# Attention values stored unscaled and loaded by pairs of heads, in a kernel of two graph-attention layers

## The chip, the cores and the metric

The kernel runs on one core of one Trainium2 chip. The metric is the device time of one execution in microseconds (us), lower is better. The profile is that of one execution; its span is a little shorter than the timed figure.

## The reference, cut to what matters

For each of B = 8 batches of N = 2048 nodes with D = 256 features there are two layers. Layer 0 has H = 8 heads of DH = 32 features:

```python
x_proj = einsum('bnd,hdf->bhnf', x, W)
e = leaky_relu(e_src[..., :, None] + e_dst[..., None, :], 0.2) + beta * log(prior + EPS)
e = where(adj > 0, e, neg_inf)
h = einsum('bhij,bhjf->bhif', softmax(e, axis=-1), x_proj)   # heads joined to 256 features
x = layernorm(x + h @ W_out.T)
```

Here `prior` is the adjacency matrix itself. Layer 1 takes `h1 = x W1`, `h2 = x W2`, `h3 = x W3`, scores `h1 h2^T` with a leaky relu, the same mask and a softmax, and ends with `layernorm(x + relu(attention h3))`.

## The kernel before, in words

**Layer 0** (class `Gat`, one object for each batch) turns the softmax into products. With the sender score split into two exponentials, kept as the factors `re` (two for each node and head), and a query row `c` for each head, the unnormalised weight of sender j for all 2048 receivers is one VectorE instruction, `s = max(c, re0[j]) * mt[j]` (L374), times a factor `re1[j]`. `mt` is a row of the transposed mask and prior, 1 MB for a tile of 128 senders. Before the change the factor `re1` is multiplied into the values v in advance (`scale`, L290 to L294: one instruction for four tiles of senders, four for a batch); the denominators take it as the weight of their product.

The work of a batch is 64 steps (`step`, L350): four pairs of heads `hp`, and in each 16 tiles of senders `jt`. A step makes two scores tiles s (buffers for two steps), and then the matrix products, L406, `val += v^T s` and `den += re1^T s`, each 16 matmuls in the profile. The denominators can also be summed on the other engines: for the tiles in the table `SUMMED` (L68, the chain of a pair) the first is copied times its factor to `d` by ScalarE (L391), the others are added on VectorE in the next step, two instructions for a tile (L385), and one product with ones brings `d` into `den` at the pair's last tile. The `d` tiles have two buffers, which the odd `mt` rows of batch 0 and its reciprocals `rb` also use.

`finish` (L410 on) copies a pair's sums out, takes reciprocals `rc`, sends them through memory (`rec_d`), reads them back spread over partitions (`rb`, L442) and multiplies (L448). `output` (L451) makes the rows of layer 0's result (`y`, L475, added to the input rows `xg` on VectorE at L477), and `turn` transposes them for layer 1.

**Layer 1** (class `Dot`) takes the rows in 16 steps of 128 (`step`, L547): scores `e` (L536), the mask on VectorE (L541), an exponential on ScalarE (L544), transposes `pt` (L559) copied to `pts` by ScalarE (L561), and the product `acc` (L575). For batch 0 it makes the mask rows `pen` from the adjacency matrix (`adj_r`, L213) and stores them; later batches load them.

**The order.** Batch 0's 64 attention steps run first, and between them the projections of batches 2, 3, 4, 5, 1, 6, 7 (`others`, L605): 16 rows a batch, in groups of four, `row` (L265) with a ScalarE copy into v (L272). After a batch's last row come its `factors` (L276) and its first `scale`, the other three at the next turns of the loop; the profile shows them close together. Batches 2 to 7 then store v as one 2 MB transfer (`store`, L296); batch 1 keeps its v in SBUF. After that, for each batch b, the attention steps of b + 1 are woven with layer 1 of b by an order written out by hand (L670 on): the last two dot steps of the batch before, with steps 0 to 5 of the new batch; the output rows and their turning, with steps 6 to 15; then 14 dot steps with the rest. At the head of a batch its v comes back in four loads (`load`, L308), into one buffer of 16 KB a partition, so after the last val product of the batch before.

TensorE's order is the program's from the start, SyncE's (SP, which issues nearly all loads and stores, in order) from L668 on. VectorE and ScalarE take their instructions in an order that the scheduler fixes at compile time, near that of the program. The `mt` rows are loaded two steps ahead (`load_ahead`, L324). The buffers `ht` (three, 4 KB a partition) hold in turn `adj_r`, `dn`, `rb`, `xg`, the transposed input `xt` and `h1`.

Of the kernel before, what the change touches and what calls it, by code (L numbers as in the profile page):

```python
# [18 lines left out]
P = 128  # L19
# [8 lines left out]
def kernel(  # L28
# [38 lines left out]

    SUMMED = [[()] * NP, [(9, 11, 13)] + [(0, 3, 6, 8, 11, 14)] * (NP - 1)]  # L68
    SUMMED += [[(8, 10, 12, 14)] + [tuple(range(0, NT, 2))] * (NP - 1)] * (B - 2)

# [88 lines left out]
    c_d = dram.tile([B, H, N], F32, name="c_d")  # L159
    v_d = dram.tile([B, P, NT, D], F32, name="v_d")  # L160
    re_d = dram.tile([B, P, 2, NT, H], F32, name="re_d")
# [43 lines left out]
    def mask(it, make):  # L205

        pen = wide_tile("pen", "pen", 1, BF16)
        if not make:
            nc.sync.dma_start(pen, pen_d[ts(it, P), :])
            return pen  # L210
        for s in range(2):
            a = chunk.tile([P, HALF], I32, tag="ht", name="adj_r", bufs=3)
            nc.sync.dma_start(a, adj[ts(it, P), ts(s, HALF)])  # L213
            nc.vector.tensor_scalar(pen[:, ts(s, HALF)], a, 0.0, NO_EDGE, ALU.is_le, ALU.mult)
        return pen
# [18 lines left out]
    class Gat:  # L234


        def __init__(self, b):
            self.b = b
            self.units = ((hp, jt) for hp in range(NP) for jt in range(NT))
            self.ms, self.mts = [], []  # L240
            self.later = gats[b - 1].later if b > 0 else []

        def begin(self, kept):


            self.v = whole.tile([P, NT, D], F32, tag=kept, name="v")
            self.both = small.tile([P, NT, 2 * H], F32, name="both", bufs=2)
# [16 lines left out]

        def row(self, it, xt, scores=True):  # L265

            cols = D + 2 * H if scores else D
            t = mm_tile("proj")
            for kc in range(KC):
                nc.tensor.matmul(t[:, 0:cols], xt[:, kc, ts(it % IG, P)], wp[:, kc, 0:cols],  # L270
                                 start=(kc == 0), stop=(kc == KC - 1))
            nc.scalar.copy(self.v[:, it, :], t[:, 0:D])  # L272
            if scores:
                nc.scalar.copy(self.both[:, it, :], t[:, D:cols])
# [14 lines left out]

        def scale(self, g):  # L290

            v = self.v[:, ts(g, IG), :].rearrange("p t (h f) -> p (t h) f", f=DH)
            e = self.re[:, 1, ts(g, IG), :].rearrange("p t h -> p (t h)")
            nc.vector.tensor_tensor(v, v, e.unsqueeze(2).to_broadcast([P, IG * H, DH]), ALU.mult)  # L294

        def store(self):  # L296
            nc.sync.dma_start(v_d[self.b], self.v)
            nc.sync.dma_start(re_d[self.b], self.re)

# [7 lines left out]

        def load(self):  # L308
            self.v = whole.tile([P, NT, D], F32, name="v")
            for g in range(NB):  # L310
                nc.sync.dma_start(self.v[:, ts(g, IG), :], v_d[self.b, :, ts(g, IG), :])
                yield

# [10 lines left out]
        def load_ahead(self):  # L324


            self.mt_loads = (load_mt(jt, False) for _ in range(self.b, B) for _ in range(NP) for jt in range(NT))
            self.c_loads = (gats[b].query_rows(h) for b in range(self.b, B) for h in range(H))
            self.mts, self.cs_ahead = [], []
            for _ in range(2):  # L330
                self.cs_ahead.append(next(self.c_loads))
                self.mts.append(next(self.mt_loads))
            self.cs_ahead.append(next(self.c_loads))

# [12 lines left out]
        def step(self, count=1):  # L347

            for _ in range(count):
                hp, jt = next(self.units)  # L350
                for work in list(self.later):
                    if next(work, self) is self:
                        self.later.remove(work)
                if self.b > 0 and hp == NP - 1 and jt == 0 and self.b + 1 < B:
                    gats[self.b + 1].load_factors()
                if jt == 0:
                    if self.b > 0:
                        self.cs = [self.cs_ahead.pop(0) for _ in range(HP)]
                    else:
                        self.cs = [self.query_rows(hp * HP + a) for a in range(HP)]  # L360
                    self.val = pacc.tile([P, HALF], F32, tag="val", name="val")
                    self.den = pacc.tile([P, HALF], F32, tag="den", name="den")
# [8 lines left out]
                for a in range(HP):  # L371
# [4 lines left out]
                    if self.b > 0 and jt == NT - 1:  # L376
                        self.cs_ahead += [c for c in [next(self.c_loads, None)] if c]
                if self.b > 0:
                    self.mts += [t for t in [next(self.mt_loads, None)] if t]
                v, e = self.v, self.re[:, 1]  # L380
                heads = [hp * HP + a for a in range(HP)]
# [4 lines left out]
                self.last = s  # L386
                self.products(self.val, [v[:, jt, ts(h, DH)] for h in heads], s, jt == 0, jt == NT - 1)
                if jt in chain[:1]:
# [21 lines left out]
        def finish(self, hp):  # L410
# [7 lines left out]
            for s in range(2):  # L418
                nc.scalar.copy(ht[lo:lo + HP * DH, ts(s, NT // 2), :],
                               self.val[ts(s, HP * DH), :].rearrange("p (t i) -> p t i", i=P))  # L420
            dn = chunk.tile([P, HALF], F32, tag="ht", name="dn", bufs=3)
            nc.scalar.copy(dn, self.den)
# [13 lines left out]
            for s in range(2):  # L436
                if b == 0:
                    rb = wide_tile("rb", "d", 2)[:, 0:HALF]
                else:
                    rb = chunk.tile([P, HALF], F32, tag="ht", name="rb", bufs=3)  # L440
                for a in range(2 * HP):
                    nc.sync.dma_start(rb[ts(a, DH), :],  # L442
                                      rec_d[b, hp // 2, s, a // HP, a % HP:a % HP + 1, :].to_broadcast([DH, HALF]))
                rbs.append(rb)
                yield
# [5 lines left out]
        def output(self):  # L451
# [6 lines left out]
            def load(g):  # L458
                xs.append(chunk.tile([P, IG, D], F32, tag="ht", name="xg", bufs=3))
                nc.sync.dma_start(xs[g], xb[:, ts(g, IG), :])  # L460

            load(0)
            yield
            for g in range(NB):
                if g < NB - 1:
                    load(g + 1)

# [45 lines left out]
    class Dot:  # L513
# [7 lines left out]
        def queries(self, g):  # L521
            self.h1 = h1 = chunk.tile([P, KC, BK], F32, tag="ht", name="h1", bufs=3)
            for dc in range(KC):
# [65 lines left out]
    g0 = gats[0]  # L589
    g0.begin("x1t")  # L590
    xt0 = whole.tile([P, KC, N], F32, tag="heads", name="xt0")
# [4 lines left out]
    for g in range(NB):  # L596
        for k in range(IG):
            g0.row(g * IG + k, xt0[:, :, ts(g, BK)], False)
        g0.scale(g)
        if g == 0:  # L600
            g0.queries()
        elif g == 1:
            g0.more_mt(1)

    def others():  # L605


# [8 lines left out]
        def turn(n):  # L616
            if n < len(groups):
                xts.append(chunk.tile([P, KC, BK], F32, tag="ht", name="xt", bufs=3))
                transpose_x(xgs[n], xts[n])
                load(n + 1)  # L620
# [4 lines left out]
        for n, (gat, g) in enumerate(groups):  # L625
            if g == 0:
                if gat is order[-1]:

                    for _ in range(IG):
                        if scaling:  # L630
                            scaling.pop(0)()
                        yield
                gat.begin("h3" if n // NB % 2 or gat is order[-1] else "v")
            for k in range(IG):
                gat.row(g * IG + k, xts[n])
                if k == 1:
                    turn(n + 1)
                if g == NB - 1 and k == IG - 1:
                    gat.factors()
                    gat.scale(0)  # L640
                    scaling.extend([lambda gat=gat, i=i: gat.scale(i) for i in range(1, NB)])
                    if gat.b > 1:
                        scaling.append(gat.store)
                if g == 0 and k == IG - 1 and n > 0:
                    groups[n - 1][0].queries()
                yield
        order[-1].queries()
        yield

    scaling = []  # L650
    projections, weights = others(), later_weights()
    next(projections)
    count = (B - 1) * NT + IG
    for k in range(1, NP * NT + 1):
# [3 lines left out]
        if k % 2 == 0:  # L658
            for _ in range(k * count // (NP * NT) - (k - 2) * count // (NP * NT)):
                next(projections)  # L660
            if scaling:
                scaling.pop(0)()
            if k > NT:
# [6 lines left out]
    for b in range(1, B + 1):  # L670
# [6 lines left out]
        if b > 1 and fresh:  # L677
            fresh.follow(gat)
            values = fresh.load()
            next(values)  # L680
            fresh.later.append(values)
        rows, turns = gat.output(), gat.turn()
        if dot is None:
            for _ in range(4):
                layer_0(1)
                if scaling:
                    scaling.pop(0)()
            next(projections)
# [61 lines left out]
```

## Time and profile before

Three timed runs took 4340.97 to 4343.44 us, median 4342.68. The profiled execution has a span of 4341.2 us and took 4343.01.

| Engine | busy us | share of the span |
|---|---|---|
| TensorE (PE) | 4208.8 | 97% |
| TensorE weight loads (PEld) | 2204.3 | 51% |
| VectorE (DVE) | 3717.5 | 86% |
| ScalarE (ACT) | 1664.9 | 38% |

| Group of instructions | count | busy us | mean ns of one |
|---|---|---|---|
| L374 s, DVE | 1024 | 2355.9 | 2344 |
| L406 val, PE | 8192 | 1043.5 | 604 |
| L385 d, DVE | 322 | 747.8 | 2343 |
| L406 den, PE (weights `re`) | 5168 | 667.1 | 597 |
| L391 d, ACT | 56 | 112.3 | 2012 |
| L294 v scaled, DVE | 32 | 37.8 | 1220 |

A mean of one instruction is from its start to its end; PE's matmuls are pipelined and overlap, so their mean is longer than their share of the engine. SP issues 496 loads of `mt` of 1 MB, six stores of v of 2 MB and 24 loads of v of 0.5 MB; the DMA engines move 839.04 MB, 193 GB/s over the span.

### The profile page before, as it was taken

What the parts mean: (1) busy time and instruction counts of PE and PEld (TensorE: products, weight loads), DVE (VectorE), ACT (ScalarE), POOL (GpSimd) and SP (SyncE); (2) the same over time, 40 slices, a digit from 0 to 9 for tenths busy, and PEclk for the clock granted to TensorE, in tenths of its full rate; (3) what the DMA queues carried; (4) which work ended last, traced back from release to release, by engine and by line L of the source; (5) the groups of instructions that cost most, each with busy time, mean ns of one, the idle gap of its engine ahead of it and who ended that gap; (6) DMA issues with size and microseconds to landing.
All of it is one profiled execution on the core that took longest, in us unless ns stands there. A gap on an engine that the chain in (4) does not pass through costs nothing. (4 is left out here: it accounts for less than half of the span.)

```text
span 4341.2 us, 58763 instructions
## 1 busy us (share of the span) xinstructions
PE 4208.8 (97%) x24608; PEld 2204.3 (51%) x24608; DVE 3717.5 (86%) x2472; ACT 1664.9 (38%) x3021; POOL 9.5 (0%) x14
## 2 busy tenths in 40 slices
PE   7999899999999999999999999999999999999999
PEld 4444345454555545555455554555455545555766
DVE  6888788898899988999899988999899988999222
ACT  6522143233343324333443333333334333333554
POOL 0000000000000000000000000000000000000000
PEclk9999999999999999999999999999999999999999
DMA  8877665566555564556555465556545565544211
GB/s 250 291 262 278 219 229 199 195 228 236 188 188 187 191 231 156 194 186 223 200 184 180 181 232 180 188 192 218 205 166 187 186 229 182 195 177 146 80 50 40
DMA packets 253162, 839.04 MB, mean 193 GB/s; under 512 B 32224, under 2 KB 150752, under 8 KB 178400
## 3 DMA queue, kind: packets, MB, share of 16 engines
q1 hardware_dynamic: 217568, 801.71, 52.3%
q10 hardware_dynamic: 35328, 33.56, 2.3%
q8 instruction: 193, 3.16, 0.3%
q14 instruction: 73, 0.60, 0.0%
HBM read 761.53 MB, written 73.14 MB: 192 GB/s over the span
## 5 line engine op out<-in xcount | busy, mean ns | idle before, releaser
L374 DVE SCALAR_TENSOR_TENSOR s<-c,re,mt 128x2048 f32<-128x2048 f32 x1024 | 2355.9, 2344 | 126.7 <-PE den L406 70.7
L406 PE MATMUL val<-s,v 128*32 128x512 f32 x8192 | 1043.5, 604 | 72.9 <-DVE s L374 72.6
L575 PE MATMUL acc<-h,pts 128*128 128x256 f32 x4096 | 955.3, 381 | 11.6 <-ACT pts L561 11.4
L536 PE MATMUL e<-x1t,h 128*128 128x512 f32 x2048 | 904.0, 594 | 4.3 <-ACT pts L561 4.2
L575 PEld LDWEIGHTS acc<-h,pts 128*128 128x128 f32 x4096 | 746.9, 190 | 110.0 <-ACT pts L561 24.4
L385 DVE SCALAR_TENSOR_TENSOR d<-s,re,d 128x2048 f32<-128x2048 f32 x322 | 747.8, 2343 | 0.0
L406 PE MATMUL den<-s,re 128*32 128x512 f32 x5168 | 667.1, 597 | 0.0
L536 PEld LDWEIGHTS e<-x1t,h 128*128 128x128 f32 x2048 | 379.0, 190 | 451.3 <-issue 414.0
L406 PEld LDWEIGHTS val<-s,v 128*32 128x32 f32 x8192 | 246.6, 110 | 709.6 <-issue 517.5
L561 ACT COPY pts<-pt 128x512 f32<-128x512 f32 x512 | 296.7, 583 | 721.8 <-PE pt L559 717.1
L538 ACT ACTIVATE p<-e 128x512 f32<-128x512 f32 x512 | 302.4, 595 | 418.4 <-PE e L536 406.6
L541 DVE CUSTOM_DVE_ANT_0 p<-p,pen 128x2048 f32<-128x2048 f32 x128 | 292.7, 2287 | 186.7 <-ACT p L538 186.2
L406 PEld LDWEIGHTS den<-s,re 128*32 128x32 f32 x5168 | 183.4, 111 | 393.9 <-issue 389.9
L559 PEld LDWEIGHTS pt<-ident,p 128*128 128x128 f32 x2048 | 238.5, 141 | 214.4 <-issue 173.1
L544 ACT ACTIVATE p<-p,neg 128x2048 f32<-128x2048 f32 x128 | 256.7, 2005 | 211.9 <-DVE neg L541 211.9
L559 PE MATMUL pt<-ident,p 128*128 128x128 f32 x2048 | 317.7, 278 | 0.0
L580 ACT ACTIVATE z<-acc,rec 128x256 f32<-128x256 f32 x128 | 60.6, 474 | 385.2 <-PE acc L575 258.8
L581 DVE TENSOR_TENSOR z<-z,x1r 128x256 f32<-128x256 f32 x128 | 54.0, 422 | 154.2 <-ACT z L580 154.2
L270 PE MATMUL proj<-wp,xt 128*128 128x272 f32 (+1 forms) x512 | 130.9, 401 | 3.4 <-ACT v L272 2.3
L272 ACT COPY v<-proj 128x256 f32<-128x256 f32 x128 | 46.9, 376 | 206.9 <-PE proj L270 193.0
L391 ACT ACTIVATE d<-s,re 128x2048 f32<-128x2048 f32 x56 | 112.3, 2012 | 33.3 <-DVE s L374 18.3
L506 PE MATMUL h3p<-w3s,x1t 128*128 128x256 f32 x512 | 122.3, 382 | 1.8 <-ACT x1t L501 1.6
(88 smaller groups left out, 1916.2 us busy)
## 6 DMA issues: line engine op xcount, KB each, us to landing
mt<-mt_d SPq DMA_DIRECT2D x496, 1024.0 KB
c<-c_d SPq DMA_DIRECT2D x64, 1024.0 KB
pen<-pen_d SPq DMA_DIRECT2D x112, 512.0 KB
xg<-in_x_dram SPq DMA_DIRECT2D x60, 512.0 KB
adj_t<-in_adj_dram SPq DMA_DIRECT2D x16, 1024.0 KB
mt_d<-mt SPq DMA_DIRECT2D x16, 1024.0 KB
rb<-rec_d SPq DMA_DIRECT2D x128, 128.0 KB
x_d<-ht ACTq DMA_DIRECT2D x32, 512.0 KB
```

Source lines behind the costliest of these rows:

```text
L270: nc.tensor.matmul(t[:, 0:cols], xt[:, kc, ts(it % IG, P)], wp[:, kc, 0:cols], start=(kc == 0), stop=(kc == KC - 1))
L374: nc.vector.scalar_tensor_tensor(sa, self.cs[a], self.re[:, 0, jt, h:h + 1], mt, ALU.max, ALU.mult)
L385: nc.vector.scalar_tensor_tensor(d, sa, e[:, jt - 1, h:h + 1], d, ALU.mult, ALU.add)
L406: nc.tensor.matmul(dst[ts(q, DH), ts(c, BK)], weights[q % 2], s[q % 2][:, ds(q // 2 * HALF + c * BK, BK)], start=start, stop=stop)
L506: nc.tensor.matmul(t[:, ts(i, D)], x1t[:, kc, ts(2 * (j - lag) + i, P)], w3s[:, kc, :], start=(kc == 0), stop=(kc == KC - 1))
L536: nc.tensor.matmul(t, self.h1[:, kc, ts(it % IG, P)], self.x1t[:, kc, ts(c, BK)], start=(kc == 0), stop=(kc == KC - 1))
L538: nc.scalar.activation(p[:, ts(c, BK)], t, AF.Prelu, alpha=ALPHA)
L541: nc.vector.tensor_tensor_reduce(p, p, pen, -1.0, FMAX, ALU.add, ALU.min, neg)
L544: nc.scalar.activation(p, p, AF.Exp, bias=neg, scale=-1.0, accum_out=den)
L559: nc.tensor.transpose(t[:, ts(k, P)], p[:, ts(g * IG + k, P)], ident)
L561: nc.scalar.copy(pt, t)
L575: nc.tensor.matmul(acc, now[:, ts(k, P)], self.h3[:, j, :], start=(j == 0), stop=(j == NT - 1))
```

## The change

The values stay unscaled when they are made. All of batches 1 to 7 are stored group by group (0.5 MB for four tiles, in the layout pair, node, tile, feature) and their factors too; the values come back by pairs of heads (0.5 MB each), at tile 4 of the pair in front, and are scaled in one instruction at tile 12 of it. Batch 0's stay in SBUF in the new layout: its first pair is scaled before the steps start, the others at tile 12 of the pair in front. The value tiles are now 4 KB a partition with three buffers; the 4 KB saved are a fourth `ht` buffer, and `output` loads its input rows two groups ahead. The chain of the first pair is taken away for batch 1 and lies on tiles 2, 4, 10, 13 for batches 2 to 7. In batch 1's first pair the odd `mt` rows go into the two `d` buffers, so that up to four rows are ahead.

```diff
-    SUMMED = [[()] * NP, [(9, 11, 13)] + [(0, 3, 6, 8, 11, 14)] * (NP - 1)]
-    SUMMED += [[(8, 10, 12, 14)] + [tuple(range(0, NT, 2))] * (NP - 1)] * (B - 2)
+    SUMMED = [[()] * NP, [()] + [(0, 3, 6, 8, 11, 14)] * (NP - 1)]
+    SUMMED += [[(2, 4, 10, 13)] + [tuple(range(0, NT, 2))] * (NP - 1)] * (B - 2)
...
-    v_d = dram.tile([B, P, NT, D], F32, name="v_d")
+    v_d = dram.tile([B, NP, P, NT, HP * DH], F32, name="v_d")
...
-            a = chunk.tile([P, HALF], I32, tag="ht", name="adj_r", bufs=3)
+            a = chunk.tile([P, HALF], I32, tag="ht", name="adj_r", bufs=4)
...
-            nc.scalar.copy(self.v[:, it, :], t[:, 0:D])
+            nc.scalar.copy(v, t[:, 0:D].rearrange("p (h f) -> p h f", h=NP))
...
-        def scale(self, g):
-
-            v = self.v[:, ts(g, IG), :].rearrange("p t (h f) -> p (t h) f", f=DH)
-            e = self.re[:, 1, ts(g, IG), :].rearrange("p t h -> p (t h)")
-            nc.vector.tensor_tensor(v, v, e.unsqueeze(2).to_broadcast([P, IG * H, DH]), ALU.mult)
-
-        def store(self):
-            nc.sync.dma_start(v_d[self.b], self.v)
-            nc.sync.dma_start(re_d[self.b], self.re)
+        def scale(self, hp):
+
+            v = self.v[hp].rearrange("p t (a f) -> p t a f", a=HP)
+            e = self.re[:, 1, :, ts(hp, HP)]
+            nc.vector.tensor_tensor(v, v, e.unsqueeze(3).to_broadcast([P, NT, HP, DH]), ALU.mult)
...
-        def load(self):
-            self.v = whole.tile([P, NT, D], F32, name="v")
-            for g in range(NB):
-                nc.sync.dma_start(self.v[:, ts(g, IG), :], v_d[self.b, :, ts(g, IG), :])
-                yield
+        def load(self, hp):
+            self.v[hp] = chunk.tile([P, NT, HP * DH], F32, tag="v", name="v", bufs=3)
+            nc.sync.dma_start(self.v[hp], v_d[self.b, hp])
...
-            self.mt_loads = (load_mt(jt, False) for _ in range(self.b, B) for _ in range(NP) for jt in range(NT))
+            self.mt_loads = (load_mt(jt, b == self.b and hp == 0)
+                             for b in range(self.b, B) for hp in range(NP) for jt in range(NT))
...
+                at = self.b * NP + hp + 1
+                if at < B * NP:
+                    gat = gats[at // NP]
+                    if jt == 4 and gat.b > 0:
+                        gat.load(at % NP)
+                    elif jt == 12:
+                        gat.scale(at % NP)
...
-                if self.b > 0:
+                if self.b > 0 and len(self.mts) < (4 if not SUMMED[self.b][hp] and jt < NT - 4 else 2):
                     self.mts += [t for t in [next(self.mt_loads, None)] if t]
...
             load(0)
+            load(1)
             yield
             for g in range(NB):
-                if g < NB - 1:
-                    load(g + 1)
+                if g < NB - 2:
+                    load(g + 2)
...
+                if k == IG - 1:
+                    nc.sync.dma_start(v_d[gat.b].rearrange("h p t f -> p h t f")[:, :, ts(g, IG), :], v)
                 if g == NB - 1 and k == IG - 1:
                     gat.factors()
-                    gat.scale(0)
-                    scaling.extend([lambda gat=gat, i=i: gat.scale(i) for i in range(1, NB)])
-                    if gat.b > 1:
-                        scaling.append(gat.store)
+                    nc.sync.dma_start(re_d[gat.b], gat.re)
...
-            values = fresh.load()
-            next(values)
-            fresh.later.append(values)
```

## The prediction

> **What bounds the kernel now.** I read the page first: TensorE (PE) is busy for 4208.8 of 4341.2 us, VectorE (DVE) for 3717.5. Then I asked for busy time by stage. Its columns are the stretch, its length, and busy us of PE, weight loads, DVE, ACT and POOL, then the granted clock, the DMA share and GB/s.
>
> ```profile
> 0.00:490.00 490.00, 443.30 (x3159) 226.11 (x3163) 400.74 (x237) 204.34 (x448) 9.49 (x14) 0.97 0.78 266
> 490.00:600.00 110.00, 92.25 (x591) 40.06 (x584) 94.32 (x60) 22.27 (x41) 0.00 (x0) 0.94 0.66 227
> 2055.00:2130.00 75.00, 69.58 (x459) 35.10 (x452) 72.91 (x48) 23.17 (x41) 0.00 (x0) 1.00 0.61 217
> 2130.00:2500.00 370.00, 368.09 (x2069) 188.24 (x2068) 348.00 (x221) 145.24 (x248) 0.00 (x0) 1.00 0.50 176
> ```
>
> Three regimes. Batch 0's attention (0 to 480) leaves PE idle for 47 us of 490. At the start of batch 1's attention (490 to 600) it idles for 17.8 of 110, and DVE is as busy as PE. From batch 2 on a batch takes some 500 us, with PE idle for 7.6; 5.4 of that lies where the output rows run (2055 to 2130): there DVE is busy for 72.9 of 75. In the long stretch with the dot steps (2130 to 2500) PE is full.
>
> So I looked for the PE gaps and what ended them, in the timeline (start, length, engine, line, what; idle before and releaser in brackets). Two of five alike:
>
> ```profile
> 315.24 3.50 DVE L294 TENSOR_TENSOR v<-v,re 128x1024 f32<-128x1024 f32 x3 [0.62 <-ACT re L288]
> ...
> 319.79 1.22 DVE L294 TENSOR_TENSOR v<-v,re 128x1024 f32<-128x1024 f32 x1
> 320.92 9.13 DVE L374 SCALAR_TENSOR_TENSOR s<-c,re,mt 128x2048 f32<-128x2048 f32 x4
> 323.32 1.92 PE L406 MATMUL val<-s,v 128*32 128x512 f32 x2 [6.24 <-DVE s L374]
> ```
>
> ```profile
> 489.86 4.63 DVE L294 TENSOR_TENSOR v<-v,re 128x1024 f32<-128x1024 f32 x4 [0.36 <-ACT re L288]
> ...
> 494.41 9.13 DVE L374 SCALAR_TENSOR_TENSOR s<-c,re,mt 128x2048 f32<-128x2048 f32 x4
> 496.81 1.86 PE L406 MATMUL val<-s,v 128*32 128x512 f32 x2 [3.88 <-DVE s L374]
> 499.05 0.33 SPq L202 DMA_DIRECT2D mt<-mt_d  x1
> 499.47 0.38 SPq L297 DMA_DIRECT2D v_d<-v  x1
> ...
> 514.28 1.23 DVE L448 TENSOR_TENSOR ht<-ht,rb 128x1024 f32<-128x1024 f32 x1 [4.14 <-DMA rb<-rec_d]
> ```
>
> Four scales of a batch come in a row on DVE, the scores s stand behind them, and PE waits for s. The second shows more: the 2 MB store of the values enters the queue ahead of the reciprocals rb, and DVE then waits 4.14 us for rb.
>
> **What the Trainium skill says.** "Perfetto Trace Analysis", Identifying the Most-Contended Engine: matmul busy time is no measure of the distance to the roof. So here: in the timeline 16 val matmuls take 1.92 us in one place and 2.99 at 2116.13, so PE loses somewhat more than its idle time shows. The same page, Optimization Strategy: a kernel can have several regimes, each read from its own gaps; the table above agrees. "VectorE: DVE Perf Modes", the perf-mode tier table: an fp32 tensor_tensor in SBUF has only the 1x rate, 2293 ns for 2048 elements, thus half for 1024; the trace has 1220 ns for L294. "DMA: Bandwidth & Descriptors", Specifications: from 512 B a packet runs at line rate. The new stores have rows of 1 KB; in this trace packets of 1 KB took 50 ns and of 8 KB 360, about the same per byte.
>
> **The change, part by part.** The sum is against the profiled span, 4341.2; the timed median, 4342.68, is 1.5 above it.
>
> *Scaling moved.* 32 scales at L294 (1220 ns) go; 32 of the same size and operation come, one for each pair of heads, at tile 12 of the pair in front. DVE's sum is the same, but 28 leave batch 0's stage, 3 stay there singly, and every batch of attention has 4. There the gain is the PE gaps behind bursts, each at most as long as the scales before it: 2.96 at 42.8 (two scales, less the one still needed: take 1.2), 2.82 at 146.7 (all), 6.24 at 317.1 (4 x 1.22 = 4.9), 4.18 at 434.7 (all). That is 13.1; I take **-12**, between -6 and -16, since another wait may stand behind. The three single scales are hidden: DVE waited there 31.2 us for PE to free score buffers.
>
> *Stores and loads.* 28 stores of 0.5 MB replace 6 of 2 MB, 28 loads replace 24. Some 2 MB more each way, at 266 GB/s 8 us of transfer each, in stages whose DMA share is 0.78 and 0.60: nothing. Their issue (0.32 to 0.6 us each) is SP's, which mostly waits. In batch 0's stage a store can stand behind an mt load; the row copies of ACT would wait for the buffer only after two further groups (about 28 us), so 0, at worst +3. The load at tile 4 is issued past mt loads on SP; two of three value buffers are then in use, so it waits for none and holds none up: 0. It goes 8 tiles, some 60 us, ahead of its scale. The row copy (376 ns) writes four pieces; ACT is 38% busy: 0. The loads at each batch's head (L311), which waited 2.2 us for the last val, go: x1r and pen behind them ended no DVE wait, so 0.
>
> *First pair of batch 1, 490 to 600.* From DVE go 4 scales (4.6), 4 chain operations of L385 (2.343 each: 9.4), and one scale comes: 94.3 becomes 81.5. Its other idle time was 4.2 for mt, 4.9 for rb, 5.1 for y. Four mt in place of two and no 2 MB store take away the mt waits; rb now shares buffers with the odd mt, so I keep 5 for rb and 4 for y: 90.5. PE gains three den tiles and loses the ones product: 2 x 1.72 = 3.4, on 92.3, 95.7. PE is then the longer: 110 - 95.7 = **-14**; the ends are -20 (by DVE) and -4 (rb waits behind an mt load that waits for a buffer, about two s pairs, 4.7 us each). ACT loses two d copies at L391 (2.0 each), hidden.
>
> *A fourth small buffer, output two loads ahead.* No y sum waited for xg. What it can do is free SP: at 772 two adj_r loads took 10.4 us to issue, 9.1 of them waiting for a buffer that rb held, and 785 to 810 has PE gaps of 1.66, 3.95, 0.87 and 0.35. At 1025 DVE waits 3.23 for an mt queued behind such loads. I take half of the 10: **-5**, between -10 and 0.
>
> *Batches 2 to 7.* Chain tiles 8, 10, 12, 14 become 2, 4, 10, 13. PE's sum is unchanged: two den tiles move behind, two ahead. What sets the end of the output stretch is DVE up to the last s. Ahead of it came two chain pairs (10, 12); now three (4, 10, 13) and a scale: +4.69 + 1.22, and 3 x 1.22 = 3.7 from the scales in the dot stretch, if nothing absorbs them: 9.6. Against it: DVE waited for PE or for z 1.98, 1.83 and 1.97 between 2036 and 2054, and 22 us in the dot stretch; and the pair of tile 14, for which the ones product waited (two of its matmuls start 1.5 apart, at 2124.8 and 2126.3), no longer stands at the end. ACT's copies at tile 2 (4 us) come among dot steps; in the other pairs such copies go with pts waits of at most 0.7. I take **0** a batch, between -3 and +4: -18 to +24 in all.
>
> Sum: -12 - 14 - 5 + 0 = -31, so 4310 as a span, **4311** timed.
>
> **The rivals.** (a) The output stretch was DVE's, and the moved chain frees it: the 4.3 + 0.9 us of PE waits at 2055 to 2130 shrink by 3 in each of six batches: 4311 - 18 = 4293. For it: DVE at 97% there. Against it: no chain pair leaves the time before the last s. (b) The shared d buffers turn the saved waits at 490 to 600 into a new one, mt behind rb on SP; that stage gives 4 rather than 14, and the small buffer nothing: 4311 + 15 = 4326. (c) The change moves DVE work from a stage with spare time into one that is nearly full: the three chain pairs and four scales before the last s of batches 2 to 7 are not absorbed. Price 9.6 - 1.5 = 8.1 a batch, 49 in all: 4360, slower. It decides the sign from 31 / 6 = 5.2 us a batch. For it: DVE 72.9 of 75, and the 348 of 370 after. Against it: DVE's waits for free score buffers just before, which show that it runs ahead. (d) Stores and loads hold up SP: against it, 0.5 MB with a free buffer.
>
> **How the numbers follow.** Likeliest 0.58; (a) 0.14; (b) 0.12; (c) and (d), in full or in part, 0.16, of which 0.07 ends within 0.2% (8.7 us, about what a measurement of this kernel can tell from no change) and 0.09 slower. So faster 0.84, same 0.07, slower 0.09. The range reaches down past (a) to 4285 and up into a half of (c) at 4335.
>
> **What would show it.** Right: no run of four value scales in the changed timeline, PE idle in 0 to 490 near 35 rather than 47, the first pair of batch 1 some 14 us shorter, 500 us a batch after. Wrong: a long DVE wait for rb or mt at 490 to 600; PE waiting for s more than 5 us in the output stretch of a later batch, or at all in its dot stretch; SP held at the value load.

## The result, and the profile after

The changed kernel takes 4319.51 us (median of four runs, 4315.73 to 4320.91), the kernel before 4341.83 beside it. The ratio is 0.9948, 95% interval 0.993 to 0.9965: faster by 22.3 us. The profiled execution has a span of 4317.4 us, 23.8 less than before. The forecast was 4311, in a range from 4285 to 4335.

The same stages of the changed kernel, by busy time (columns as before):

```profile
0.00:490.00 490.00, 452.51 (x3282) 230.29 (x3282) 392.01 (x221) 204.38 (x449) 9.49 (x14) 0.99 0.85 286
490.00:600.00 110.00, 103.68 (x630) 51.46 (x627) 86.58 (x62) 35.11 (x60) 0.00 (x0) 0.97 0.65 230
```

```profile
2020.50:2095.50 75.00, 69.37 (x458) 35.62 (x457) 69.59 (x47) 20.96 (x42) 0.00 (x0) 0.98 0.61 215
2095.50:2465.50 370.00, 364.91 (x2050) 185.23 (x2049) 346.74 (x222) 141.79 (x244) 0.00 (x0) 1.00 0.50 179
```

The last two are laid against the same pair ends as 2055 to 2130 and 2130 to 2500 before. PE idles for 37.5 us of the first 490 (46.7 before) and 6.3 of the next 110 (17.8 before), but for 5.1 of the 370 with the dot steps (1.9 before), which were said to be full. The first two stretches also hold more work than before, since the changed kernel is ahead. So for the account I cut both kernels where ScalarE starts to copy a pair's sums (`ht<-val`), which ends each pair of heads:

| Stretch | before, us | after, us | change | predicted |
|---|---|---|---|---|
| batch 0 | 480.4 | 462.9 | -17.5 | -12 |
| batch 1, first pair | 120.9 | 106.1 | -14.8 | -14 |
| batch 1, third pair, and batch 2, first pair | 261.4 | 249.0 | -12.4 | -5 |
| batch 1, second and fourth pair | 268.1 | 269.9 | +1.8 | 0 |
| the rest of batch 2, and batches 3 to 7 | 2878.5 | 2897.3 | +18.8 | 0 |
| after the last pair | 331.9 | 332.0 | +0.1 | 0 |

A batch in the steady part had pairs of 120.0 (121.7 in batches 5 and 7), 138.2, 119.8 and 121.2 us; now they have 120.5 to 121.6, 139.0, 120.9 and 122.3, some 3 us more in all. In batch 7 the fourth pair, which has no later values to scale, still takes 121.2.

**Where batch 0's time came from.** All 32 scales now come alone (1199 to 1225 ns each), and no instruction waited for one. At the place where the four scales of batch 2 had held PE up for 6.24 us, the timeline of the changed kernel has this (start, length, engine, line, what; idle before and releaser):

```profile
307.57 4.62 DVE L375 SCALAR_TENSOR_TENSOR s<-c,re,mt 128x2048 f32<-128x2048 f32 x2 [5.55 <-DMA mt<-mt_d]
...
309.98 1.04 PE L407 MATMUL val<-s,v 128*32 128x512 f32 x2 [2.02 <-DVE s L375]
...
312.24 2.78 PE L407 MATMUL val<-s,v 128*32 128x512 f32 x11 [1.22 <-DVE s L375]
```

Another wait did stand behind, for an mt row, but it costs PE 3.2 us rather than 6.2. A second effect is seen in slices of 5 us (third last column: the granted TensorE clock; third: PE busy). Before:

```profile
315.00:320.00 5.00, 2.08 (x20) 0.39 (x12) 4.76 (x5) 0.21 (x2) 0.00 (x0) 0.94 0.84 339
320.00:325.00 5.00, 1.68 (x2) 0.18 (x2) 5.00 (x3) 0.00 (x0) 0.00 (x0) 0.50 0.87 331
325.00:330.00 5.00, 4.65 (x25) 1.10 (x27) 5.00 (x3) 0.00 (x0) 0.00 (x0) 0.53 0.84 323
330.00:335.00 5.00, 5.00 (x31) 3.28 (x24) 3.79 (x3) 1.96 (x6) 0.00 (x0) 1.00 0.04 8
```

After:

```profile
305.00:310.00 5.00, 2.98 (x29) 0.67 (x21) 2.42 (x2) 0.00 (x0) 0.00 (x0) 1.00 1.01 385
310.00:315.00 5.00, 3.78 (x18) 0.91 (x22) 4.28 (x2) 0.00 (x0) 0.00 (x0) 0.68 1.00 423
```

The gap is followed by a stretch at half clock, and PE's 6.3 busy us at 0.50 and 0.53 hold the work of 3.3. What PE did in the first of these two slices would at any clock have had to wait for the second score, which PE could take up at 325.59; in the other slice 4.65 busy us at 0.53 hold the work of 2.5. So I estimate that the gap of 6.24 cost some 2 us more than its length. The Trainium skill, "TensorE: Matmul & The Clock Gate", Part 1: The HAM clock gate, says that an idle window of about 3.4 us takes the clock to half; the gap of 6.24 agrees, but the 0.68 in the changed kernel follows two gaps of only 2.02 and 1.22 us, so less was enough here. Over batch 0 PE made the same 3091 matmul records in 433.70 busy us before and 427.43 after: of the 17.5, 11.2 are idle time and 6.3 are busy time. By the clock records of the two traces the clock stood at 0.50 for 27.3 us of batch 0 before and for 13.7 after; half of the difference, 6.8 us, is the most that this can have cost, so the 6.3 fit the clock.

**The fourth small buffer.** In the third pair of batch 1 PE had such a gap too, of 3.95 us at 799.6, with half clock behind it. One of the waits of SyncE's queue there, before (us in total, times, longest):

```profile
SPq L213 <- DVE ht L448: 9.1, 1, 9.1
```

(L213 loads `adj_r`; it waits for the multiplication at L448, which reads `rb`, to free a small buffer), and in five-us slices of that kernel just behind it:

```profile
800.00:805.00 5.00, 1.39 (x2) 0.14 (x2) 4.80 (x5) 1.52 (x6) 0.00 (x0) 0.91 0.07 26
805.00:810.00 5.00, 4.17 (x16) 0.77 (x16) 5.00 (x3) 0.00 (x0) 0.00 (x0) 0.50 0.62 210
```

The 9.1 us at L213 are gone after. PE's waits for s in this pair fall from 6.8 to 1.5 us, and its busy time from 127.28 (granted clock 0.97) to 123.09 (1.00): together the 9.5 us that the pair became shorter.

**What the later batches lost.** PE's waits in batches 4 to 7 (us in total, times, longest), before, after, and in the changed kernel with the old chain (experiment 2 below):

```profile
PE val L406 <- DVE s L374: 17.1, 20, 2.1
PE acc L575 <- ACT pts L561: 5.8, 16, 0.6
PE den L406 <- DVE d L385: 3.5, 4, 0.9
```

```profile
PE val L407 <- DVE s L375: 26.4, 20, 3.3
PE acc L577 <- ACT pts L563: 9.0, 19, 0.8
PE h1p L528 <- ACT x1t L503: 6.0, 4, 1.5
```

```profile
PE val L407 <- DVE s L375: 20.8, 24, 2.2
PE acc L577 <- ACT pts L563: 9.0, 19, 0.8
PE den L407 <- DVE d L386: 3.5, 4, 0.9
```

These four batches took 2000.2, 2011.4 and 2005.7 us. The waits explain the whole of the second difference to before: with the old chain val and acc wait for 6.9 us more, and the time is 5.5 longer. The moved chain takes away the wait of `den` for `d`, 0.9 a batch as foreseen, and brings 1.4 a batch at val (experiment 5 shows from where) and 1.5 at h1p. The last one is seen in the timeline of the changed kernel, at the start of a second pair:

```profile
2092.56 2.00 ACT L392 ACTIVATE d<-s,re 128x2048 f32<-128x2048 f32 x1 [10.82 <-PE den L407]
...
2094.47 2.01 ACT L420 COPY ht<-val 64x1024 f32<-64x1024 f32 x2
...
2097.40 0.59 ACT L503 COPY x1t<-tr 128x512 f32<-128x512 f32 x1
...
2098.05 1.98 PE L528 MATMUL h1p<-x1t,w 128*128 128x512 f32 x4 [1.49 <-ACT x1t L503]
```

and of the kernel before:

```profile
2129.14 2.02 ACT L419 COPY ht<-val 64x1024 f32<-64x1024 f32 x2
...
2131.18 0.58 ACT L501 COPY x1t<-tr 128x512 f32<-128x512 f32 x1
...
2132.14 2.02 ACT L391 ACTIVATE d<-s,re 128x2048 f32<-128x2048 f32 x1
```

In both, the 2 us copy to `d` of the pair's first tile is in ScalarE's order near the copies of the pair that ended. The compile-time order put it behind `x1t` before and ahead of it after, so PE's h1p stood 1.49 us for x1t. ScalarE had been idle for 10.82 us and is 38% busy: it is the order, not the load.

The scales' part is seen when the dot stretch of the kernel before is cut by pairs, the second, third and fourth of batch 4 (the third busy time: DVE):

```profile
2129.10:2267.40 138.30, 138.03 (x747) 72.47 (x749) 124.58 (x81) 55.44 (x96) 0.00 (x0) 1.00 0.48 171
2267.40:2387.20 119.80, 119.10 (x684) 58.76 (x677) 116.16 (x71) 45.68 (x80) 0.00 (x0) 1.00 0.54 183
2387.20:2508.30 121.10, 120.17 (x712) 62.79 (x708) 116.46 (x74) 46.08 (x77) 0.00 (x0) 1.00 0.51 184
```

DVE is busy for 90% of the second pair (and of the first, 108.52 of 120), but for 97% and 96% of the third and fourth. The 22 us of the whole stretch lie mostly in its first pair.

**Why the first pair varies.** Batches 4 and 5 of the kernel before run the same steps, and in the first pair of both PE waits 2.09 us for s, from 2076.84 and from 2576.04 on. The 10 us from each of them on:

```profile
2076.80:2086.80 10.00, 7.91 (x54) 4.76 (x54) 9.55 (x7) 2.69 (x7) 0.00 (x0) 1.00 0.63 203
2576.00:2586.00 10.00, 7.91 (x43) 3.59 (x43) 7.85 (x6) 2.58 (x6) 0.00 (x0) 0.83 0.65 203
```

Behind the second wait the clock stood at 0.50 for 3.41 us, behind the first it stayed at 1.00, and PE's 7.91 busy us hold 43 matmul records behind the second wait and 54 behind the first. Batch 4's first pair took 120.0, batch 5's 121.7. It is the same in all kernels below that have this wait of 2.09 to 2.15 us: where no half clock follows, the first pair takes 120.0 to 120.3 in batches 3 to 7, and 121.7 where 3.41 us of it follow. So the length of a gap does not alone decide whether the clock falls.

### The profile page after: what moved, and what is told of

Read it like the earlier page. It is cut to its first block, busy times and chain, and to the rows that moved or that the text cites. A ratio compares the mean times of both kernels' runs of the same rounds, so it can differ in the third digit from the quotient of the medians.

```text
span 4317.4 us, 58896 instructions
## 1 busy us (share of the span) xinstructions
PE 4191.7 (97%) x24640; PEld 2202.1 (51%) x24640; DVE 3704.8 (86%) x2468; ACT 1657.5 (38%) x3019; POOL 9.5 (0%) x14
## 5 line engine op out<-in xcount | busy, mean ns | idle before, releaser
L407 PE MATMUL val<-s,v 128*32 128x512 f32 x8192 | 1024.5, 602 | 56.7 <-DVE s L375 56.5
L386 DVE SCALAR_TENSOR_TENSOR d<-s,re,d 128x2048 f32<-128x2048 f32 x318 | 738.5, 2342 | 0.0
L528 PE MATMUL h1p<-x1t,w 128*128 128x512 f32 x256 | 117.0, 595 | 9.4 <-ACT x1t L503 9.4
```

What stands on the lines that cost most here:

```text
L386: nc.vector.scalar_tensor_tensor(d, sa, e[:, jt - 1, h:h + 1], d, ALU.mult, ALU.add)
L407: nc.tensor.matmul(dst[ts(q, DH), ts(c, BK)], weights[q % 2], s[q % 2][:, ds(q // 2 * HALF + c * BK, BK)], start=start, stop=stop)
L528: nc.tensor.matmul(t, w12[:, kc, ts(dc, P)], self.x1t[:, kc, ts(g, BK)], start=(kc == 0), stop=(kc == KC - 1))
```

## The experiments

Each kernel is compared with the kernel before, run beside it: 4345.3, 4346.33, 4344.9 and 4345.04 us in the four groups below. "Pair" durations are of the profiled execution. Batch 0 runs the same steps in all of these kernels and still took between 462.2 and 467.9 us, so a few us in a span stay unexplained by any edit; a pair of the steady part repeats to some tenths, except the first, which is some 1.7 us longer where the clock fell in it.

**1. Scales left out.** No scale in front of the second to fourth pair of batches 2 to 7.

```diff
-                    elif jt == 12:
+                    elif jt == 12 and not (gat.b > 1 and at % NP):
```

> The changed kernel without the scales of pairs 1 to 3 of batches 2 to 7 (18 instructions of 1.22 us left out; the values of these pairs stay unscaled). Theory A (in the stretch with dot steps each scale pushes the mask operation back by about its own length, so the exponential comes ahead of a pts copy on ScalarE and PE's acc waits): pairs 2 and 3 of each of these batches lose the 1.1 us that they gained over the kernel before, pair 1, whose loss comes from a d copy, keeps it: about 2.2 x 6 = 13 less, some 4306 us. Rival B (VectorE's sum is the bound there, every pair costs its 1.2): all three pairs shorten, about 20 less, 4299. Rival C (the value loads at tile 4 or their DMA are what costs): no change, 4319.

Measured: 4311.47 us, ratio 0.9923 (0.9908 to 0.9937). A scale runs in the pair in front of its own, which the expectation had one pair too late: those left out lie in the first three pairs. The third pair went from 120.9 to 119.8, the second stayed at 139.0, the first at 120.8 to 121.6. The fourth kept its scale, for the next batch, and its 122.3. So a scale costs nothing in the first and second pair, and 1.1 of its 1.21 us in the third; from batch 7's fourth pair, which has none, the same in the fourth.

**2. The old chain** for the first pairs of batches 2 to 7, all else as changed.

```diff
-    SUMMED += [[(2, 4, 10, 13)] + [tuple(range(0, NT, 2))] * (NP - 1)] * (B - 2)
+    SUMMED += [[(8, 10, 12, 14)] + [tuple(range(0, NT, 2))] * (NP - 1)] * (B - 2)
```

> The changed kernel with the first pair's chain of batches 2 to 7 back on tiles 8, 10, 12, 14. Theory A (with the chain ended at tile 13 the next pair's first d copy is put ahead of the x1t copy on ScalarE, and PE's h1p waits 1.5 us; against it the output stretch is about 1 us shorter): h1p no longer waits, the output stretch is 1 to 2 us longer, a batch is within 1 us of now, 4313 to 4325 us. Rival B (moving the chain is what makes room for the scale at tile 12 in the output stretch): the first pair of each batch grows by 2.5 to 4, 4334 to 4343.

Measured: 4313.13, ratio 0.9924 (0.9909 to 0.9939). The second pair is back at 138.2, the first at 120.2 to 120.4: with rows loaded two groups ahead the moved chain is a loss of some 1.5 us a batch, and nothing of the output stretch was freed.

**3. Three small buffers,** with output rows loaded one group ahead, since two ahead want the fourth.

```diff
-            a = chunk.tile([P, HALF], I32, tag="ht", name="adj_r", bufs=4)
+            a = chunk.tile([P, HALF], I32, tag="ht", name="adj_r", bufs=3)
...
-            load(1)
...
-                if g < NB - 2:
-                    load(g + 2)
+                if g < NB - 1:
+                    load(g + 1)
```

> The changed kernel with three ht buffers and output loading one group ahead, as before. Theory A (the fourth buffer frees SP in batch 1, where adj_r loads waited for buffers): pair 2 of batch 1 grows from 124.7 us back to about 134 and the first pair of batch 2 by about 3, in all 4319 + 12 = 4331. Rival B (these gains come from the values no longer loaded at the head of the batch and from other alignment): within 2 us, 4317 to 4321.

Measured: 4321.88, ratio 0.9944 (0.9928 to 0.9961), not told apart from the changed kernel. But the pairs moved both ways: batch 1's third 134.3 (124.7 with four), batch 2's first 129.9 (124.3), batch 1's first 101.2 (106.1), the steady first 119.6 (120.5 to 121.6). The buffer gives 15 us, and loading two groups ahead seemed to take them back.

**4. Batch 1's first pair as before:** chain on tiles 9, 11, 13 and two mt rows ahead.

```diff
-    SUMMED = [[()] * NP, [()] + [(0, 3, 6, 8, 11, 14)] * (NP - 1)]
+    SUMMED = [[()] * NP, [(9, 11, 13)] + [(0, 3, 6, 8, 11, 14)] * (NP - 1)]
...
-            self.mt_loads = (load_mt(jt, b == self.b and hp == 0)
+            self.mt_loads = (load_mt(jt, False)
...
-            for _ in range(3):
+            for _ in range(2):
...
```

> The changed kernel with batch 1's first pair as before: chain on tiles 9, 11, 13 and mt rows two ahead, none in the d buffers. Theory A (of the 14.8 us that this pair became shorter, the four scales and the 2 MB store give about 5 and the chain and the deeper mt loads about 10): that pair grows from 106 to about 116 us, 4329 in all. Rival B (the burst of scales and the store were all of it): that pair stays under 109, 4319 to 4322. Rival C (the rows loaded deeper are harmful, rb behind them): shorter than 106.

Measured: 4329.5, ratio 0.9961 (0.9946 to 0.9976). That pair takes 111.8 (106.1 as changed, 120.9 before). So most of its gain, 9.1 of 14.8, stays without the chain's removal and the deeper rows, and 5.7 comes from these two.

The next four were run to part these further.

**5. Output rows one group ahead,** four small buffers.

```diff
-            load(1)
...
-                if g < NB - 2:
-                    load(g + 2)
+                if g < NB - 1:
+                    load(g + 1)
```

> The changed kernel with four ht buffers kept and output loading its rows one group ahead, as before. Theory A (the two parts of the buffer edit act apart: the fourth buffer made pair 2 of batch 1 and the first pair of batch 2 shorter, the loads two ahead made the first pairs longer): the first pair of batch 1 near 101 us and of batches 3 to 7 near 119.6 as with three buffers, pair 2 of batch 1 near 125, the first pair of batch 2 near 123 or less; the span 12 less than the changed kernel, about 4305. Rival B (the fourth buffer itself lengthens the first pairs, by another placement or order): first pairs as in the changed kernel, 106 and 121, about 4317.

Measured: 4308.96, ratio 0.9912 (0.9895 to 0.9928). Batch 1's first pair takes 101.9, the steady first pair 119.6 in four of five batches, batch 1's third still 124.7. The buffer is the gain, the earlier loads are a loss. In batch 1's first pair VectorE's order shows why. In the changed kernel an addition of output rows stands ahead of the next score and waits for TensorE's `y`:

```profile
509.18 0.69 DVE L479 TENSOR_TENSOR ht<-y,xg 128x512 f32<-128x512 f32 x1 [3.31 <-PE y L477]
...
511.51 2.34 DVE L375 SCALAR_TENSOR_TENSOR s<-c,re,mt 128x2048 f32<-128x2048 f32 x1
```

In this one three scores come first, and the additions behind them don't wait:

```profile
509.62 6.87 DVE L375 SCALAR_TENSOR_TENSOR s<-c,re,mt 128x2048 f32<-128x2048 f32 x3
516.41 1.28 DVE L478 TENSOR_TENSOR ht<-y,xg 128x512 f32<-128x512 f32 x2
```

PE, which waits for these scores, has a gap of 3.04 us in the changed kernel and of 2.10 at most here. The slices of the changed kernel, and the whole pair of this one:

```profile
510.00:515.00 5.00, 1.96 (x7) 0.59 (x5) 4.70 (x5) 0.47 (x2) 0.00 (x0) 0.82 1.00 400
515.00:520.00 5.00, 4.05 (x17) 0.80 (x20) 5.00 (x4) 2.12 (x5) 0.00 (x0) 0.50 0.82 297
```

```profile
466.60:568.50 101.90, 95.69 (x692) 45.03 (x685) 89.65 (x61) 24.58 (x53) 0.37 (x1) 1.00 0.70 255
```

PE's waits for s differ by 1.8 us in this pair (7.7 and 5.9), its busy time by 2.6. No addition waited for `xg` in either kernel. So the two timelines put the loss down to VectorE's compile-time order, which this edit also changes, and not to the queue of loads; no run holds the order fixed. In the steady first pairs it is alike: in batch 4 of the changed kernel two additions, one of which waits 1.01 us for `y`, and their statistics stand ahead of a score for which PE waits 3.26 us; here PE's longest wait is 1.82.

**6. Both: one group ahead and the old chain** (the edits of 2 and 5).

> The same with the first pair's chain of batches 2 to 7 back on tiles 8, 10, 12, 14. Theory A (the loads ahead and the moved chain cost separately): what either gave alone adds, pair 1 at 138.2, first pairs 119 to 120, about 8 less than with one group ahead alone, some 4297. Rival B (both removed the same wait): no better than the better of the two, about 4305.

Measured: 4303.89, ratio 0.9904 (0.9889 to 0.9919): faster than both kernels of this study. Its steady pairs are 120.0, 138.2, 120.9 and 122.3. It leaves the scales as the only loss against before. What the two edits gave alone does not add up, so the rival is the nearer one: with rows one group ahead the moved chain costs only 0.3 us a batch (501.8 in kernel 5, 501.5 here, where the clock did not fall), since it makes the second pair 0.8 longer and the first 0.4 shorter.

**7. Kernel 6 with the scales at tile 14.**

```diff
-                    elif jt == 12:
+                    elif jt == 14:
```

> The same again with the scale at tile 14 in place of tile 12. Theory A (the 1.1 us in pairs 2 and 3 come from the scale standing ahead of the mask operation at one place of the order): with the scale elsewhere these pairs go to 119.8 and 121.2 or change by another amount, pair by pair: -13 at best against the kernel with the scale at tile 12, some 4284. Rival B (VectorE is full there and any tile costs the same 1.1): unchanged, 4297.

Measured: 4307.59, ratio 0.9908 (0.9894 to 0.9923); third and fourth pair unchanged at 120.9 and 122.3. In the third pair the scale moved by 15.8 us; in the fourth it stayed where it was, near tile 7: VectorE's compile-time order does not follow the written tile there, so for that pair nothing was tested. In the third pair another tile cost the same.

**8. The values alone:** the old chains, two mt rows, three small buffers, output one ahead.

```diff
-    SUMMED = [[()] * NP, [()] + [(0, 3, 6, 8, 11, 14)] * (NP - 1)]
-    SUMMED += [[(2, 4, 10, 13)] + [tuple(range(0, NT, 2))] * (NP - 1)] * (B - 2)
+    SUMMED = [[()] * NP, [(9, 11, 13)] + [(0, 3, 6, 8, 11, 14)] * (NP - 1)]
+    SUMMED += [[(8, 10, 12, 14)] + [tuple(range(0, NT, 2))] * (NP - 1)] * (B - 2)
...
```

> The kernel before with the values' part of the change alone: stored unscaled, loaded and scaled by pairs; old chains, three ht buffers, output one ahead, mt rows two ahead. Theory A (the values' part gives the 17.5 us of batch 0 and some 9 of the first pair of batch 1, and costs 1.1 in each of pairs 2 and 3 of batches 2 to 7, 12 or 13 in all; nothing in the rest): 4341 - 17.5 - 9 + 13 = 4328. Rival B (the part gains nothing without the buffers and chains): 4341 or more.

Measured: 4327.82, ratio 0.9954 (0.994 to 0.9969). Batch 0 466.8, batch 1's first pair 109.6, its third 133.7 (134.2 before): the values give -13.6 and -11.3 and cost 2.2 us a batch later. The third pair's gain is not theirs.

The last three and a fourth ask whether the scales' price can be had back, and what the deeper rows are worth.

**9. Kernel 6 with values loaded two pairs ahead and scaled at tile 2.**

```diff
-                    if jt == 4 and gat.b > 0:
...
-                    elif jt == 12:
+                    if jt == 4 and self.b > 0 and at + 1 < B * NP:
+                        gats[(at + 1) // NP].load((at + 1) % NP)
+                    if jt == (12 if self.b == 0 or first_pair else 2):
```

> The kernel with the old chain and output one group ahead; from batch 1 on the values are loaded two pairs ahead and scaled at tile 2 of the pair in front, before the place where VectorE waits at the pair's start. Theory A (VectorE runs without a break from the first third of pairs 2 and 3 to the place where PE or the mask waits for it; a scale ahead of its last break is hidden): pair 2 at 119.8 and pair 3 at 121.2, as before the change, 13 less in all. Rival B (VectorE's sum is the bound, each scale costs 1.1 wherever it is): 120.9 and 122.3. Rival C (the order that the scheduler fixes is changed elsewhere): other lengths, in pair 1 too.

Measured: 4307.85, ratio 0.9917 (0.99 to 0.9933). The third pair is back at 119.8, the fourth stays at 122.3. VectorE's order did not put the scales where they are written: a steady batch has one in its first pair, one in the second, none in the third and two in the fourth, 10 and 57 us after its start. So the third pair is shorter because no scale is left in it, and the second scale of the fourth pair cost nothing there. There is no gain in sum: in four of batches 2 to 7 the clock fell in the first pair (121.7 to 122.1, else 120.0), and batch 1 takes 500.9 us, 4.0 more than in kernel 6.

**10. Kernel 6 with the scale on GpSimd.**

```diff
-            nc.vector.tensor_tensor(v, v, e.unsqueeze(3).to_broadcast([P, NT, HP, DH]), ALU.mult)
+            nc.gpsimd.tensor_tensor(v, v, e.unsqueeze(3).to_broadcast([P, NT, HP, DH]), ALU.mult)
```

> The same kernel with the scale on GpSimd in place of VectorE, at tile 12. Theory A (the 1.1 us in pairs 2 and 3 are VectorE's time): both go back to 119.8 and 121.2, pair 1 stays at 138.2, 13 less in all, if GpSimd is done before the next pair's first val and does not slow VectorE. Rival B (the two engines hold each other up while they read and write SBUF): s instructions beside it take longer than 2.34 us and the pairs keep their length.

Measured: 4328.6, ratio 0.9964 (0.9951 to 0.9977), slower than with VectorE. The timeline shows a scale on GpSimd beside two scores:

```profile
2389.02 2.42 POOL L292 TENSOR_TENSOR v<-v,re 128x1024 f32<-128x1024 f32 x1 [114.44 <-DMA v<-v_d]
...
2389.57 6.28 DVE L375 SCALAR_TENSOR_TENSOR s<-c,re,mt 128x2048 f32<-128x2048 f32 x2
```

Two scores take 4.60 us elsewhere: here they took 1.7 longer, more than the 1.21 of the scale saved. Over batch 5 VectorE's busy time is 472.01 us; in kernel 6 it is 470.28, with four scales more on it. Against kernel 6 a steady batch is 3.5 us longer, of which 1.7 is the half clock, which here came in the first pair of all batches from 2 on; the other pairs are 0.8, 0.6 and 0.5 longer. The Trainium skill, "SBUF — State Buffer", Who interferes with whom, says that a VectorE instruction with two inputs in SBUF contends with a GpSimd instruction that reads SBUF; the two lines agree.

**11. Kernel 6 with two mt rows ahead** in batch 1's first pair, without its chain.

```diff
-            self.mt_loads = (load_mt(jt, b == self.b and hp == 0)
+            self.mt_loads = (load_mt(jt, False)
...
-                if self.b > 0 and len(self.mts) < (4 if not SUMMED[self.b][hp] and jt < NT - 4 else 2):
+                if self.b > 0 and len(self.mts) < 2:
```

> The kernel with the old chain for batches 2 to 7 and output one group ahead, with batch 1's first pair without a chain (as changed) but mt rows two ahead and none in the d buffers. Theory A (the missing chain is what made that pair shorter beyond the scales and the store; the deeper loads add little, since the 2 MB store that delayed them is gone): 103 to 105 us. Rival B (the deeper loads gave it): 107 to 110, as with the chain and two ahead (109.6 in the values-alone kernel).

Measured: 4312.26, ratio 0.9927 (0.9912 to 0.9941). The pair takes 108.7: 103.4 with deeper rows, 109.6 with the chain too (kernel 8, which also has three small buffers). So the rows give some 5 us, the chain's removal about 1. But VectorE waits only 0.9 us for mt in kernel 11. It waits 4.5 us for `y` (0.7 in kernel 6), in the order of experiment 5's first timeline; PE waits 3.1 us more for s, and its busy time is 2.3 longer. Row depth and VectorE's order changed together here, and what the depth gives by itself is not shown.

**12. Kernel 6 with the early scale in the third pair only.**

```diff
+                    early = self.b > 0 and hp == NP - 2
-                    if jt == 4 and gat.b > 0:
+                    if jt == 4 and gat.b > 0 and not early:
...
-                    elif jt == 12:
+                    if jt == 4 and self.b > 0 and hp == NP - 3:
+                        gat.load(NP - 1)
+                    if jt == (2 if early else 12):
```

> The kernel with the old chain and output loads one ahead, and in every batch after batch 0 the values of the fourth pair are loaded one pair earlier (at tile 4 of the second pair) and scaled at tile 2 of the third pair instead of tile 12; all other scales stay at tile 12. Theory A (in the third pair VectorE pays the 1.1 us because the scale at tile 12 falls where it has no lead over TensorE; at tile 2 it has): the third pair of batches 2 to 7 goes from 120.9 to 119.8 us, the first pair stays at 120.0 because its scales are untouched, the others stay at 138.2 and 122.3; 7 x 1.1 = 8 us less than 4304, so 4296, ratio to the kernel before 0.989. Theory B (the 1.1 saved in the third pair comes back in the first pair, as it did when all scales were at tile 2, where first pairs were 121.7 to 122.1 in four of five batches): third pair 119.8, first pair 121.1 or more, ratio 0.990 to 0.992, about 4304 to 4310.

Measured: 4302.37, ratio 0.9904 (0.9887 to 0.992), the same ratio as kernel 6. The third pair is 119.8 in all batches from 2 on, as the first theory has it. But VectorE's order put its scale into the second pair, just behind that pair's own, and the second pair is 139.0 in place of 138.2: 0.8 of the 1.1 comes back there. The first is 121.7 in two of batches 3 to 7, the two in which the clock fell, so not for the second theory's reason. This kernel and kernel 6 cannot be told apart.

## Why the prediction was right, and where it was off

The direction and the mechanism hold, and the time is 8.5 us above the forecast (whose own steps add up to 4311.7). By its steps:

- *Scaling moved, -12.* Right in kind: no bursts, and the other wait that "may stand behind" is there (mt, 3.2 us at 310). Too small: each gap was counted at its own length, but the half clock after it costs too: 6.3 of the 17.5 are busy time. Part of the rest is chance: in the other kernels batch 0 gains between 12.5 and 18.2.
- *Stores and loads, 0.* In the changed kernel no engine's wait is put down to the loads or stores of v; kernel 8, which has them all, loses 2.2 us a batch, and the two scales of 1.1 explain that.
- *First pair of batch 1, -14.* The number was met by two errors that cancel. The step had PE lose all its idle time there (17.8) and take 3.4 more work. It still idles for 7.9, so 9.9 are gained; and its busy time, for 27 more matmul records, went down from 103.14 to 98.32 as the clock rose from 0.94 to 0.97. The bound -4, with rb behind mt rows, did not come: DVE waits for rb no longer stand there; of what was kept for waits, the 4 for y came (3.6), the 5 for rb did not. By kernels 4, 8 and 11 the values give 9 to 11, the rows 5 (with the change of VectorE's order that came with them), the chain 1; the two-ahead loads take about 4 back.
- *Fourth small buffer, -5.* This term was mis-sized the most downward. "I take half of the 10" failed: the buffer alone gave 9.6 in the third pair and 6.4 in batch 2's first (kernel 3 against 5), and the loads two ahead, costed at nothing, took 4.2 in batch 1's first pair and, with the moved chain, 0.9 to 2.0 in most later first pairs. The ground given, that no y sum waited for xg, is true; that the edit would change VectorE's order was not looked at. What was left is -12.4 in the two pairs.
- *Batches 2 to 7, 0.* This is the term that made the time longer than forecast: +18.8, near the end of the range given (+24). DVE's waits did absorb the three chain pairs and the scale of the first pair to within 2 us a batch, and all of the second pair's scale. What failed is the reading of "22 us in the dot stretch" as spare time for all three pairs: 13.7 of it lay in the second, and in the third and fourth 1.1 of a 1.21 us scale reaches PE, some 12 of the 18.8. And of ACT's copies only those at tile 2 were weighed; it is the next pair's first copy that came in front of x1t and costs 1.49 of PE's time at h1p, though not all of it stays (the second pair is 0.8 longer, some 5 in all).
- *The rivals.* (a) is refuted by kernel 2: the moved chain frees 0.9 a batch at den and pays 2.9 at val and h1p. (b)'s wait did not come. (c) is what happened in part, 3 us a batch rather than 8.1 and below its point of decision, 5.2; its chain pairs were absorbed, half of its scales not. (d) did not come for v, and where loads did cost, for xg, the timelines show VectorE's order and not SP's queue.

Of the signs named, "PE idle near 35" (37.5) and "no run of four scales" held, "500 us a batch" did not (503), and 5.4 us of waits for s in an output stretch (first pair of batch 4) stood just past the mark set for a wrong reason. A wait of PE for s in the dot stretch, named as a sign of being wrong too, came as well: 0.7 us in the third pair, where there was none before.

What stays open: why the scheduler orders VectorE differently when only loads are moved, what deeper rows give with the order held, and what decides, beside its length, whether a gap of some 2 us takes the clock down.

## What to carry to other kernels

Price a gap on TensorE by its length and by the slow clock that can follow it: in batch 0 the gaps' removal gave 11.2 us of idle time and 6.3 of busy time. When two runs of the same steps differ, look at the clock in them before you blame an edit. Spare time of the second engine is to be read for each place where work is added, not over a stretch: with VectorE 90% busy a 1.21 us operation was free, with 96 or 97% nearly all of it reached TensorE. Even so the place within a pair counts: in kernel 9 a second scale was free near the start of the fourth pair, and in kernel 12 it was not free just behind another in the second, where VectorE is less busy. An edit of loads can change the order of an engine that they don't run on, so compare that engine's timeline before you look for the reason in the queue. Test a bundle's parts one by one: here two of five parts were losses inside a gain, and without them the change was worth 42 us rather than 22.

## What the runs showed of the hardware

- After a gap of 6.24 us on TensorE the granted clock was 0.50 and 0.53 for 10 us; after one of 3.04 it was 0.82 and then 0.50 in slices of 5 us. A gap of 2.09 us at the same place of the program was followed by 3.41 us at 0.50 in batches 5 and 7 of the kernel before, and by none in batches 3, 4 and 6; the pair was 1.7 us longer with it.
- A 128 x 1024 product took 1.94 to 6.10 us on GpSimd (median 2.52) and 1.20 to 1.23 on VectorE, and two scores running beside it took 6.28 us in place of 4.60.
- The same program's batch 0 differed by up to 5.7 us between kernels that do not differ there.
